# Two graph attention layers in one kernel: order of the first loads, four key buffers, a diagonal made by GpSimd, and the last sums split between engines

## The chip, the cores and the metric

The kernel runs on one core of a Trainium2 chip. A core has a matrix engine (TensorE, "PE" in the profile), three engines for elementwise work (VectorE "DVE", ScalarE "ACT", GpSimd "POOL"), and SyncE ("SP"), which here only starts transfers. Each engine executes its own instructions in order and waits for others by semaphores. The metric is the time of the whole kernel on the device, in microseconds; the number compared is the median of several runs.

## The reference: what is computed

Input are 4096 nodes with 512 features, `x`, and an adjacency matrix of 4096 x 4096 zeros and ones. Two layers follow each other, each with a residual and a layer normalisation.

```python
# layer 0: graph attention, 4 heads of width 128
support = (x @ weight)                       # per head
logits  = f1[None, :] + f2[:, None]          # two scalars per node and head
w       = where(logits >= 0, logits, 0.2 * logits)
masked  = w * adjacency
attn    = softmax(where(masked != 0, masked, -1e30)) * (masked != 0)
x       = layernorm(x + attn @ support + bias + x @ proj_w + proj_b)

# layer 1: masked attention, 8 heads of width 64
adj     = maximum(adjacency, eye)            # every node sees itself
q, k, v = x @ Wqs, x @ Wks, x @ Wvs          # per head
scores  = q @ k.T / 8 + 0.01 * eye - 1e16 * (1 - adj)
x       = layernorm(x + sum over heads of softmax(scores) @ v @ Wo)
```

In layer 1 the kernel takes the exponential without a maximum and multiplies by the adjacency matrix afterwards. The term `0.01 * eye` together with `maximum(adjacency, eye)` then means that the mask holds exp(0.01) = 1.01005 on its diagonal.

## The kernel before, as far as the change touches it

All matrices are float32. Constants: `P = 128`, `G = 512` queries in a group, `NG = 8` groups, `NT = 32` tiles of 128 keys, `NP1 = 4` pairs of heads, `NB = 3` key tiles in a batch. A "pair" (g, m) below is one group of queries with one pair of heads; there are 32 of them, each with 32 units j (one key tile each).

The head: loads of the first group of x, of the two weights and of the small vectors, then the transposes of x.

```python
            load_x(0)                                     # four DMAs, SyncE's queue
            for c in range(KC):
                nc.scalar.dma_start(w_sb[c], weight[c * P:(c + 1) * P, :])
            for c in range(KC):
                nc.sync.dma_start(pw_sb[c], proj_w[c * P:(c + 1) * P, :])
            nc.sync.dma_start(uv[:, 0, :], on_all_partitions(weight_u, D))
            # ... three more small vectors, each spread over all partitions
            load_x(1)
            # ...
            def turn_x(g, c):
                # ...
                p = xp.tile([P, GT, P], F32, name="x_ps")          # two such PSUM tiles
                for t in range(GT):
                    nc.tensor.transpose(p[:, t, :], xs[g * GT + t][:, c * P:(c + 1) * P], ident)  # line 701
                # copy to xT: VectorE for odd c (line 704), ScalarE for even c (line 706)

            for c in range(KC):
                turn_x(0, c)
            for g in range(NG):
                for t in range(GT):
                    # s_ps = xT @ w_sb  (line 727, 4 steps)
                    # b_ps = xT @ pw_sb (line 733, 4 steps), then turn_x(g + 1, ...)
```

During that stage GpSimd narrows the adjacency matrix to bfloat16 by DMA, SyncE's queue transposes it by DMA (`stage`), and ScalarE narrows it once more to 8 bits (line 582).

Between the layers the keys and queries are made. A PSUM tile with two heads' results is copied to `kq` (keys by VectorE, line 927; queries by ScalarE, line 929) and stored to HBM:

```python
                    kq = sp.tile([P, HP, G], F32, name="kq")       # two buffers
                    if w is wk:
                        nc.vector.tensor_copy(kq, s)
                    else:
                        nc.scalar.activation(kq, s, AF.Copy, scale=float(KD) ** -0.5)
                    # two DMAs to HBM on SyncE's queue
```

The pair loop of layer 1. In each unit TensorE makes scores (line 904), ScalarE the exponential in PSUM (line 1018), VectorE the product with the mask (line 1021), TensorE the product with the values (line 1066), and GpSimd adds the weights up for the softmax's denominator (`q_sum`):

```python
        def finish_md(g, t):          # the mask of the four tiles with the diagonal
            if t == 0:
                mdt[g] = lp.tile([P, GT, G], F32, name="md", bufs=1)
            nc.scalar.activation(mdt[g][:, t, :], mask(g, g * GT + t), AF.Copy)    # line 883
            d = mdt[g][:, t, t * P:(t + 1) * P]
            nc.vector.tensor_tensor(d, d, ident_e, op=ALU.max)                     # line 885
        # called in unit (g, 0, 4 * (g - 1) + t), used in units (g, m, 4 * g + t)

            def weigh(g, m, j, s):
                # ... exp(s) in place
                p = wp.tile([P, HP, G], F32, name="p1", bufs=18)
                keep = mdt[g][:, j % GT, :] if j // GT == g else mask(g, j)
                nc.vector.tensor_tensor(p, s, keep[:, None, :].to_broadcast([P, HP, G]), op=ALU.mult)

            def add_up(g, m, j):
                # for every second j: a, b are the weights of j - 1 and j; i = j // 2, n = 16
                if i == 0:
                    later.at(1, first)                    # q_sum = a + b, GpSimd
                elif at_end and i >= n - 2:               # at_end: the last pair (7, 3)
                    last_sum.extend((a, b))
                elif i % 8 == 7 or at_end and i >= n - 4:
                    later.at(2, lambda: add(a))           # q_sum += a, GpSimd, line 1041
                    later.at(3, lambda: add(b))
                else:
                    later.at(2, lambda: nc.gpsimd.dma_start(a, b, accum_op=ALU.add))  # a += b by DMA
                    later.at(5, lambda: add(a))
```

`later.at(n, ...)` issues an instruction n batches later. `all_sums` adds tiles over the partitions by a product with ones (line 1072), `project` is the product with `Wo` (line 1110), `close1` adds the residual (line 1120), normalises and stores. The end of the kernel:

```python
            step([], None, None)
            later.step()
            step([], None, tiles[-5], 2)
            # ... PSUM tiles y_ps[0..3], den_ps
            project(*tiles[-4], y_ps[0], range(NP1 - 1))
            all_sums([q_sum.pop(pairs[-1])] + last_sum, den_ps[:, 0, :])   # q_sum and four tiles
            divide_at_once(*pairs[-1], den_ps[:, 0, :])     # reciprocals by VectorE, line 1102
            for n in range(GT):
                if n + 1 < GT:
                    project(*tiles[n + 1 - GT], y_ps[n + 1], range(NP1 - 1))
                project(*tiles[n - GT], y_ps[n], [NP1 - 1])
                # ... close1
```

Of the kernel before, what the change touches and what calls it, by code (L numbers as in the profile page):

```python
# [8 lines left out]
F32 = mybir.dt.float32  # L9
# [4 lines left out]
ALU = mybir.AluOpType  # L14
# [4 lines left out]
P = 128  # L19
# [410 lines left out]
def tile_gat_then_masked_attention(  # L430
# [16 lines left out]
    nc = tc.nc  # L447
# [4 lines left out]
    G = 512  # L452
    NG = N // G
    GT = G // P
# [24 lines left out]
    nc.gpsimd.memset(minus_half, -0.5)  # L479
    ones = const.tile([P, KD], F32, name="ones")  # L480
    nc.gpsimd.memset(ones, 1.0)
    ident_e = const.tile([P, P], F32, name="ident_e")
    nc.vector.tensor_scalar(ident_e, ident, 1.0100501670841679, None, op0=ALU.mult)
    most = const.tile([P, NG * NP1], F32, name="most")
    total = const.tile([P, NG * NP1], F32, name="total")

# [64 lines left out]
    with tc.tile_pool(name="l0", bufs=NG) as l0, \  # L551
# [71 lines left out]
        with tc.tile_pool(name="l0s", bufs=2) as sp:  # L623
# [11 lines left out]

            load_x(0)
            for c in range(KC):
                nc.scalar.dma_start(w_sb[c], weight[c * P:(c + 1) * P, :])
            for c in range(KC):
                nc.sync.dma_start(pw_sb[c], proj_w[c * P:(c + 1) * P, :])  # L640
            nc.sync.dma_start(uv[:, 0, :], on_all_partitions(weight_u, D))
            nc.sync.dma_start(uv[:, 1, :], on_all_partitions(weight_v, D))
            nc.sync.dma_start(bb[:, 0, :], on_all_partitions(bias, D))
# [51 lines left out]
            def turn_x(g, c):  # L695

                if c == 0:
                    xTs[g] = sp.tile([P, KC, G], F32, name="xT")
                p = xp.tile([P, GT, P], F32, name="x_ps")
                for t in range(GT):  # L700
                    nc.tensor.transpose(p[:, t, :], xs[g * GT + t][:, c * P:(c + 1) * P], ident)
                dst = xTs[g][:, c, :]
                if c % 2:
                    nc.vector.tensor_copy(dst, p.rearrange("p t r -> p (t r)"))  # L704
                else:
                    nc.scalar.activation(dst, p.rearrange("p t r -> p (t r)"), AF.Copy)

            for c in range(KC):
                turn_x(0, c)
            for g in range(NG):  # L710
                xg = [xs[g * GT + t] for t in range(GT)]
                xT = xTs.pop(g)
                if g == 0:
                    nc.gpsimd.tensor_add(bb[:, 0, :], bb[:, 0, :], bb[:, 1, :])
                for t in range(GT):
                    nc.gpsimd.tensor_tensor(xg[t], xg[t], bb[:, 0, :], op=ALU.add)
                fs[g] = l0.tile([P, 2, GT, H0], F32, name="f")
                s4 = sp.tile([P, GT, H0, W0], F32, name="s4")
                for t in range(GT):
                    i = g * GT + t  # L720
                    if t == 1 and g + 2 < NG:
                        load_x(g + 2)
                    for fn in beside.get(i, []):
                        fn()
                    s_ps = op.tile([P, G], F32, name="o_ps")
                    for c in range(KC):
                        nc.tensor.matmul(s_ps, xT[:, c, t * P:(t + 1) * P], w_sb[c],  # L727
                                         start=(c == 0), stop=(c == KC - 1))
                    if g + 1 < NG and t == GT - 1:
                        turn_x(g + 1, t)  # L730
                    b_ps = op.tile([P, G], F32, name="o_ps")
                    for c in range(KC):
                        nc.tensor.matmul(b_ps, xT[:, c, t * P:(t + 1) * P], pw_sb[c],
                                         start=(c == 0), stop=(c == KC - 1))
                    if g + 1 < NG and t < GT - 1:
                        turn_x(g + 1, t)
                    nc.scalar.activation(s4[:, t, :, 0:D0],
                                         s_ps.rearrange("p (h d) -> p h d", h=H0), AF.Copy)
                    for k in range(2):
                        prod = sp.tile([P, H0, D0], F32, name="prod")  # L740
                        nc.vector.tensor_tensor(prod, s4[:, t, :, 0:D0],
                                                uv[:, k, :].rearrange("p (h d) -> p h d", h=H0),
                                                op=ALU.mult)
                        nc.vector.tensor_reduce(fs[g][:, k, t, :], prod, AX.X, ALU.add)
                    base = sp.tile([P, D], F32, name="base", bufs=4)
                    nc.vector.tensor_tensor(base, b_ps, xg[t], op=ALU.add)
                    nc.sync.dma_start(base_d[i], base)
                    later.step()
                factors(g, s4)
# [115 lines left out]
    with wait_by_tile("l1", 1) as l1, wait_by_tile("l1a", 2) as lp, \  # L865
# [13 lines left out]
        def finish_md(g, t):  # L879

            if t == 0:
                mdt[g] = lp.tile([P, GT, G], F32, name="md", bufs=1)
            nc.scalar.activation(mdt[g][:, t, :], mask(g, g * GT + t), AF.Copy)
            d = mdt[g][:, t, t * P:(t + 1) * P]
            nc.vector.tensor_tensor(d, d, ident_e, op=ALU.max)  # L885

        def load_kv(g, m, c):
            kt[g, m, c] = lp.tile([P, 2 * G], F32, name="k_sb", bufs=3)
# [21 lines left out]
        with wait_by_tile("l1s", 2) as sp:  # L910
# [7 lines left out]
            def keys_or_queries(g, w, dst):  # L918
                for m in range(0, NP1, 2):
                    s = ps.tile([P, HP, G], F32, name="s_ps")  # L920
                    for n in range(2):
                        for c in range(KC):
                            nc.tensor.matmul(s[:, n, :], w[:, c, (m + n) * P:(m + n + 1) * P],  # L923
                                             xTs[g][:, c, :], start=(c == 0), stop=(c == KC - 1))
                    kq = sp.tile([P, HP, G], F32, name="kq")
                    if w is wk:
                        nc.vector.tensor_copy(kq, s)
                    else:
                        nc.scalar.activation(kq, s, AF.Copy, scale=float(KD) ** -0.5)  # L929
                    for n in range(2):  # L930
                        nc.sync.dma_start(dst[m + n][g // 2][:, g % 2, :] if w is wk
                                          else dst[m + n][g], kq[:, n, :])
                    later.step()
                    later.step()
# [53 lines left out]
        with wait_by_tile("l1w", 2) as wp, wait_by_tile("l1o", 1, space=PSUM) as op:  # L988
# [4 lines left out]
            units = [(g, m, j) for g, m in pairs for j in range(NT)]  # L993
            index = {u: n for n, u in enumerate(units)}

            def loads(u):

                n = index[u]
                g, m, j = u
                if j % CH == 0:  # L1000
                    if n + CH < len(units):
                        g1, m1, j1 = units[n + CH]
                        if j1 == 0:
                            load_q(g1, m1)
                        load_kv(g1, m1, j1 // CH)
                if m == NP1 - 1 and (g + 1) * G % W == 0 and g + 1 < NG and j % CJ == 0:
                    for c in ((0, 1) if j == 0 else (j // CJ + 1,) if j // CJ + 1 < NCJ else ()):
                        load_adjT((g + 1) * G // W, c)
                if m == 0 and g and j // GT == g - 1:
                    finish_md(g, j % GT)  # L1010

            def scores(g, m, j):
                loads((g, m, j))
# [11 lines left out]
            def add_up(g, m, j):  # L1025
# [16 lines left out]

                if i == 0:
                    later.at(1, first)
                elif at_end and i >= n - 2:
                    last_sum.extend((a, b))
                elif i % 8 == 7 or at_end and i >= n - 4:
                    later.at(2, lambda: add(a))
                    later.at(3, lambda: add(b))
                else:  # L1050
                    later.at(2, lambda: nc.gpsimd.dma_start(a, b, accum_op=ALU.add))  # L1051
                    later.at(5, lambda: add(a))
# [55 lines left out]
            def project(g, t, s, ms=range(NP1)):  # L1108
                for m in ms:
                    nc.tensor.matmul(s, on_t[g][:, m, t * P:(t + 1) * P], wo_sb[:, m, :],  # L1110
                                     start=(m == 0), stop=(m == NP1 - 1))
# [62 lines left out]
                load_y(*t)  # L1174
            step([], None, None)
            later.step()
            step([], None, tiles[-5], 2)
            y_ps = ps.tile([P, HP, G], F32, name="s_ps")
            den_ps = ps.tile([P, HP, G], F32, name="s_ps")
            o_ps = op.tile([P, 2, G], F32, name="o1_ps")  # L1180
            y_ps = [y_ps[:, 0, :], y_ps[:, 1, :], o_ps[:, 0, :], o_ps[:, 1, :]]
            project(*tiles[-4], y_ps[0], range(NP1 - 1))
            all_sums([q_sum.pop(pairs[-1])] + last_sum, den_ps[:, 0, :])
            divide_at_once(*pairs[-1], den_ps[:, 0, :])
            for n in range(GT):
                if n + 1 < GT:
                    project(*tiles[n + 1 - GT], y_ps[n + 1], range(NP1 - 1))
                project(*tiles[n - GT], y_ps[n], [NP1 - 1])
                if n == GT - 2:
                    all_ok = all_in_range()  # L1190
                close1(*tiles[n - GT], y_ps[n], 1)
                later.step()
# [40 lines left out]
```

## Time and profile before

| quantity | value |
|---|---|
| time, median of 3 runs | 3474.48 us (3465.94 to 3479.73) |
| span of the profiled run | 3467.4 us |
| TensorE busy | 3421.7 us, 99% |
| VectorE busy | 2396.2 us, 69% |
| GpSimd busy | 2019.3 us, 58%; 1593.9 of 1700 us from 1600 to 3300 us |
| ScalarE busy | 1874.0 us, 54% |
| transfers | 620.8 MB, 179 GB/s on average |

How to read the lines below. A line of the busy times gives engine, busy microseconds, share of the span and number of instructions. In the list of waits a line reads: waiting engine, what it was about to do and its line, the releaser and its line; then microseconds in total, how often, and the longest. In the timeline and in the chain a line begins with start and duration; a timeline line goes on with engine, line, operation, output and input, their sizes and how many instructions were merged; in brackets stand the idle time ahead and what ended it. The kernel's stages in this run: layer 0's own products to about 249 us, its attention to 1175 us, keys, queries and values of layer 1 to about 1510 us, the pair loop to 3418 us, and the tail.

### The profile page before, as it was taken

To read this page: it belongs to the slowest core of one execution; us is meant where nothing else is said; L and a number is where in the kernel's file an instruction comes from. 1 tells how busy PE (TensorE), PEld (TensorE's weight loads), DVE (VectorE), ACT (ScalarE), POOL (GpSimd) and SP (SyncE) were. 2 spreads that over 40 slices of the span, in tenths; PEclk is the share of its full clock that TensorE was granted. 3 is DMA by queue.
4 is the path that set the end of the run, shared out by engine and by line. 5 is a ranking of instruction groups with operands and counts; after the bars stand their busy time and mean duration, and the time that the engine had idled before them with its cause. 6 is when DMAs were issued, how large, how long until landed. Compare 5 with 4: busy or idle time off the path is not lost.

```text
span 3467.4 us, 64921 instructions
## 1 busy us (share of the span) xinstructions
PE 3421.7 (99%) x26666; PEld 1867.3 (54%) x26666; DVE 2396.2 (69%) x2512; ACT 1874.0 (54%) x2194; POOL 2019.3 (58%) x1452
## 2 busy tenths in 40 slices
PE   9999999999999999999999999999999999999997
PEld 4459999999999744443333333333333333333332
DVE  3469999898898500047787777767776777767774
ACT  1236877878876310035555555555555555555552
POOL 3330031040020100039999999999999999999996
PEclk9999999999999999999999999999999999999998
DMA  8988959779441432458978988788988889787884
GB/s 185 229 176 144 211 126 217 146 172 205 141 111 62 101 130 97 161 154 196 206 182 206 243 192 205 190 207 229 214 190 207 194 199 253 190 209 187 210 190 96
DMA packets 398162, 620.80 MB, mean 179 GB/s; under 512 B 165536, under 2 KB 243616, under 8 KB 396832
## 3 DMA queue, kind: packets, MB, share of 16 engines
q0 software_dynamic: 97360, 258.50, 41.1%
q1 hardware_dynamic: 299392, 355.97, 34.9%
q8 instruction: 211, 3.46, 0.4%
q10 hardware_dynamic: 1104, 2.10, 0.2%
q14 instruction: 95, 0.78, 0.1%
HBM read 315.87 MB, written 117.64 MB: 125 GB/s over the span
## 4 chain that ended last, share of the span: by engine, by line
PE 61%; POOL 1%; DVE 1%; issue 1%; ACT 0%; DMA 0%; SPq 0%; POOLq 0%; DVEq 0%; ACTq 0%
PE s_ps L904 25%; PE o_ps L1066 24%; PE s_ps L923 5%; PE s_ps L1110 3%; PE s_ps L951 3%; PE s_ps L1072 1%; POOL q_sum L1041 1%; DVE p L1021 1%; PE x_ps L951 0%; DVE md L885 0%; ACT s_ps L1018 0%; DMA k_sb<-k_d 0%; DVE r L1086 0%; PE o_ps L1110 0%; POOL on L1090 0%
## 5 line engine op out<-in xcount | busy, mean ns | idle before, releaser
L1041 POOL TENSOR_TENSOR q_sum<-q_sum,p 128x1024 f32<-128x1024 f32 x543 | 1386.9, 2554 | 60.5 <-DMA p<-p 37.9
L1018 ACT ACTIVATE s_ps<-s_ps 128x1024 f32<-128x1024 f32 x1021 | 969.3, 1010 | 700.2 <-PE s_ps L904 698.7
L1021 DVE TENSOR_TENSOR p<-s_ps,adjT 128x1024 f32<-128x1024 f32 x896 | 1043.1, 1216 | 406.4 <-ACT s_ps L1018 389.7
L904 PE MATMUL s_ps<-q_sb,k_sb 64*64 64x512 f32 x8192 | 947.5, 590 | 7.2 <-DVE p L1021 5.9
L1066 PE MATMUL o_ps<-p,v_sb 64*64 64x512 f32 x8192 | 944.2, 590 | 0.0
L855 PE MATMUL o_ps<-sup_t,p 128*128 128x129 f32 x8192 | 919.0, 275 | 0.0
L855 PEld LDWEIGHTS o_ps<-sup_t,p 128*128 128x128 f32 x8192 | 916.8, 192 | 0.0
L618 DVE SCALAR_TENSOR_TENSOR p<-fr_t,dj,az 128x1024 f32<-128x1024 f32 x512 | 653.6, 1285 | 82.3 <-PE o_ps L855 54.9
L609 ACT ACTIVATE z<-fr_t,f 128x1024 fp8e4<-128x1024 f32 x512 | 558.4, 1144 | 126.5 <-DVE az L613 126.2
L904 PEld LDWEIGHTS s_ps<-q_sb,k_sb 64*64 64x64 f32 x8192 | 314.6, 133 | 576.8 <-issue 449.7
L1066 PEld LDWEIGHTS o_ps<-p,v_sb 64*64 64x64 f32 x8192 | 313.5, 133 | 569.7 <-issue 558.9
L1051 POOL DMA_DIRECT2D p<-p x413 | 439.3, 1299 | 24.8 <-PE o_ps L1066 15.5
L819 POOL DMA_DIRECT2D agg<-base_d x32 | 28.7, 1205 | 515.4 <-ACT agg L807 515.2
L1037 POOL TENSOR_TENSOR q_sum<-p,p 128x1024 f32<-128x1024 f32 x32 | 76.0, 2374 | 301.1 <-DVE p L1021 301.1
L1021 DVE TENSOR_TENSOR p<-s_ps,md 128x1024 f32<-128x1024 f32 x128 | 150.5, 1216 | 61.8 <-ACT s_ps L1018 60.6
L613 DVE TENSOR_TENSOR az<-adjT,z 128x512 int32<-128x512 int32 x256 | 175.5, 686 | 1.8 <-ACT z L609 1.0
L582 ACT ACTIVATE adjT<-stage 128x1024 fp8e4<-128x1024 bf16 x128 | 130.7, 1050 | 58.5 <-DMA stage<-adj_d 58.5
L569 POOL COPY seen<-token 128x1 f32<-128x1 f32 x24 | 13.5, 563 | 251.7 <-DVE token L567 251.7
L957 DVE COPY vg<-s_ps 128x512 f32<-128x512 f32 x15 | 10.4, 691 | 207.8 <-ACT vg L953 207.8
L929 ACT ACTIVATE kq<-s_ps 128x1024 f32<-128x1024 f32 x16 | 16.4, 1023 | 191.7 <-PE s_ps L923 184.5
L727 PE MATMUL o_ps<-w_sb,xT 128*128 128x512 f32 x256 | 116.3, 597 | 1.3 <-DVE xT L704 1.3
L1086 DVE RECIPROCAL r<-den 128x128 f32<-128x128 f32 x124 | 116.4, 939 | 0.0
(99 smaller groups left out, 1832.7 us busy)
## 6 DMA issues: line engine op xcount, KB each, us to landing
p<-p POOLq DMA_DIRECT2D x413, 512.0 KB, 9.1
k_sb<-k_d SPq DMA_DIRECT2D x128, 512.0 KB, 7.9
v_sb<-v_d SPq DMA_DIRECT2D x128, 512.0 KB, 6.4
adj_d<-in_adj_dram POOLq DMA_DIRECT2D x32, 1024.0 KB, 14.5
sup_t<-sup_d SPq DMA_DIRECT2D x120, 258.0 KB, 8.4
adjT_d<-adjT SPq DMA_DIRECT2D x32, 512.0 KB, 4.5
fr_t<-fr_d SPq DMA_DIRECT2D x16, 1024.0 KB, 6.6
adjT<-adjT_d SPq DMA_DIRECT2D x32, 512.0 KB, 8.1
```

Source lines behind the costliest of these rows:

```text
L582: nc.scalar.activation(adjT[w, c][:, k, :], stage[w, c][:, k, :], AF.Copy, saturate=False)
L609: nc.scalar.activation(z[:, k, :], fr[:, 0, :], AF.Sign, bias=fs[j // GT][:, 0, (j + k) % GT, h:h + 1], saturate=False)
L613: nc.vector.tensor_tensor(az.bitcast(I32), adjT[w, j // CJ][:, j % CJ:j % CJ + 2, :].bitcast(I32), z.bitcast(I32), op=ALU.bitwise_and)
L618: nc.vector.scalar_tensor_tensor(p, fr[:, 1, :], dj[j // GT][:, j % GT, h:h + 1], az_t[w, h, j // 2][:, j % 2, :], op0=ALU.max, op1=ALU.mult)
L855: nc.tensor.matmul(o[t // BK][:, t % BK, :], p[:, t * P:(t + 1) * P], s, start=(j == 0 and t % BK == 0), stop=(j == NT - 1), skip_group_ch ...
L904: nc.tensor.matmul(s[c:c + MS, e, :], k[r, a + c:a + c + MS], qt[g, m][r, :], start=True, stop=True)
L923: nc.tensor.matmul(s[:, n, :], w[:, c, (m + n) * P:(m + n + 1) * P], xTs[g][:, c, :], start=(c == 0), stop=(c == KC - 1))
L1018: nc.scalar.activation(s, s, AF.Exp)
L1021: nc.vector.tensor_tensor(p, s, keep[:, None, :].to_broadcast([P, HP, G]), op=ALU.mult)
L1041: nc.gpsimd.tensor_tensor(q, q, p, op=ALU.add)
L1051: later.at(2, lambda: nc.gpsimd.dma_start(a, b, accum_op=ALU.add))
L1066: nc.tensor.matmul(o[c, n, :], v[r, j % CH, c], p[r, e, :], start=(j == 0), stop=(j == NT - 1))
```

## The change

It has four parts. The order of the first loads: w is loaded behind x on SyncE's queue, and proj_w on ScalarE's queue behind the first copy of the transposed x; two of the first four transposes go to PSUM tiles of another pool, so that they need not wait for a copy. The keys and queries get four buffers instead of two. The diagonal of the mask is set by GpSimd's selection instead of a maximum on VectorE, and a pair of heads ahead of its first use instead of four units ahead. In the last pair, the weights of the last ten key tiles are not added by GpSimd: VectorE adds eight of them into one, TensorE takes that one and the last two, and the projections of two output tiles instead of one are issued before those sums.

```diff
-    ident_e = const.tile([P, P], F32, name="ident_e")
-    nc.vector.tensor_scalar(ident_e, ident, 1.0100501670841679, None, op0=ALU.mult)
...
             load_x(0)
             for c in range(KC):
-                nc.scalar.dma_start(w_sb[c], weight[c * P:(c + 1) * P, :])
-            for c in range(KC):
-                nc.sync.dma_start(pw_sb[c], proj_w[c * P:(c + 1) * P, :])
+                nc.sync.dma_start(w_sb[c], weight[c * P:(c + 1) * P, :])
...
-                p = xp.tile([P, GT, P], F32, name="x_ps")
+                if g == 0 and c > 1:
+                    p = op.tile([P, G], F32, name="o_ps").rearrange("p (t r) -> p t r", t=GT)
+                else:
+                    p = xp.tile([P, GT, P], F32, name="x_ps")
...
             for c in range(KC):
                 turn_x(0, c)
+                if c == 0:
+                    for n in range(KC):
+                        nc.scalar.dma_start(pw_sb[n], proj_w[n * P:(n + 1) * P, :])
...
-            nc.vector.tensor_tensor(d, d, ident_e, op=ALU.max)
+            nc.gpsimd.affine_select(out=d, in_=d, compare_op=ALU.not_equal, base=0,
+                                    fill=1.0100501670841679, pattern=[[-1, P]],
+                                    channel_multiplier=1)
...
-                    kq = sp.tile([P, HP, G], F32, name="kq")
+                    kq = sp.tile([P, HP, G], F32, name="kq", bufs=4)
...
+            diagonal = {index[g - 1, NP1 - 1, 0] + (g + 1) * GT + t: (g, t)
+                        for g in range(1, NG) for t in range(GT)}
...
-                if m == 0 and g and j // GT == g - 1:
-                    finish_md(g, j % GT)
+                if n in diagonal:
+                    finish_md(*diagonal[n])
...
-                elif at_end and i >= n - 2:
+                elif at_end and i >= n - 5:
                     last_sum.extend((a, b))
-                elif i % 8 == 7 or at_end and i >= n - 4:
+                elif i % 8 == 7:
...
             step([], None, None)
             later.step()
+            for p in last_sum[1:-2]:
+                nc.vector.tensor_tensor(last_sum[0], last_sum[0], p, op=ALU.add)
             step([], None, tiles[-5], 2)
...
-            project(*tiles[-4], y_ps[0], range(NP1 - 1))
-            all_sums([q_sum.pop(pairs[-1])] + last_sum, den_ps[:, 0, :])
+            for n in range(2):
+                project(*tiles[n - GT], y_ps[n], range(NP1 - 1))
+            all_sums([q_sum.pop(pairs[-1]), last_sum[0]] + last_sum[-2:], den_ps[:, 0, :])
             divide_at_once(*pairs[-1], den_ps[:, 0, :])
             for n in range(GT):
-                if n + 1 < GT:
-                    project(*tiles[n + 1 - GT], y_ps[n + 1], range(NP1 - 1))
+                if n + 2 < GT:
+                    project(*tiles[n + 2 - GT], y_ps[n + 2], range(NP1 - 1))
```

## The prediction

> **What bounds the kernel now.** I read the page's busy times and 40 slices first, then the list of waits of TensorE, then the chain of waits in order of time, then the timeline where those two show a hole.
>
> ```profile
> PE 3421.7 (99%) x26666; PEld 1867.3 (54%) x26666; DVE 2396.2 (69%) x2512; ACT 1874.0 (54%) x2194; POOL 2019.3 (58%) x1452
> PE s_ps L1072 <- POOL q_sum L1041: 10.9, 1, 10.9
> PE x_ps L701 <- DMA x_sb<-in_x_dram: 7.5, 4, 4.3
> PE s_ps L904 <- DVE p L1021: 5.9, 4, 3.5
> PE x_ps L836 <- ACT x1T L841: 3.8, 3, 1.9
> ```
>
> TensorE is idle for only 3467.4 - 3421.7 = 45.7 us of the span. No other engine is near that, and the change takes no matrix product away, so nothing can bring more than these 45.7 us plus what hides inside "busy" (matmuls stretched by small waits or by a lower clock). The four waits shown are the largest: the tail (10.9), the head (7.5), and two in between. The three main parts of the change aim at the first three.
>
> The 5.9 us of the third wait understate that hole. The chain in order of time has one piece per pair of heads, the projection on line 1110, and its starts give the period:
>
> ```profile
> 1852.11 3.63 PE s_ps L1110 x8
> 1911.83 3.63 PE s_ps L1110 x8
> 1971.55 3.63 PE s_ps L1110 x8
> 2033.22 3.63 PE s_ps L1110 x8
> 2092.94 3.63 PE s_ps L1110 x8
> ```
>
> The period is 59.72 us; one is 61.67, so 1.95 was lost. Followed to the end, all periods are 59.72 but for 61.67, 61.29 (from 2212.38 to 2273.67), 60.97 (from 2452.83 to 2513.80) and 60.53 (from 3170.73 to 3231.26). Before 1852 there is no projection and the period is 1677.54 - 1621.45 = 56.09; the two periods to 1796.02 take 118.48, which is 6.30 too much. Sum of the losses: 6.30 + 1.95 + 1.57 + 1.25 + 0.81 = 11.9 us. The losing pairs are those with m = 0 of groups 1, 2, 3, 4 and 7, where `finish_md` makes the diagonal mask. The worst one:
>
> ```profile
> 1736.09 6.89 DVE L885 TENSOR_TENSOR md<-md,ident_e 128x128 f32<-128x128 f32 x3
> 1739.05 8.63 POOL L1041 TENSOR_TENSOR q_sum<-q_sum,p 128x1024 f32<-128x1024 f32 x3
> 1742.90 3.47 DVE L1021 TENSOR_TENSOR p<-s_ps,adjT 128x1024 f32<-128x1024 f32 x3
> 1744.17 4.63 PE L904 MATMUL s_ps<-q_sb,k_sb 64*64 64x512 f32 x24 [3.51 <-DVE p L1021]
> ```
>
> Three maxima on 128x128 take 6.89 us, though the fastest of the 32 took 0.276. One of them ran from 1739.01 to 1742.98, beside a GpSimd sum from 1739.05 to 1742.82. VectorE stands behind it, so its masking product and TensorE's next scores are late.
>
> The tail:
>
> ```profile
> 3417.62 17.96 POOL L1041 TENSOR_TENSOR q_sum<-q_sum,p 128x1024 f32<-128x1024 f32 x7
> 3435.64 1.94 PE L1072 MATMUL s_ps<-q_sum,ones 128*32 128x512 f32 x8 [10.92 <-POOL q_sum L1041]
> 3443.16 0.96 DVE L1102 RECIPROCAL r<-s_ps 128x128 f32<-128x128 f32 x1 [19.35 <-PE s_ps L1072]
> 3453.55 0.69 DVE L1120 TENSOR_TENSOR y<-y,o_ps 128x512 f32<-128x512 f32 x1 [0.91 <-PE o_ps L1110]
> ```
>
> When the last product is issued GpSimd still has seven sums in its queue; they end at 3435.58 and TensorE waits 10.92 us.
>
> **What the skill says.** "SBUF — State Buffer", section "Who interferes with whom": a VectorE instruction with two SBUF inputs excludes a GpSimd instruction that reads SBUF, each for its whole length; with one SBUF input it does not. The trace agrees: the diagonal's maximum (two SBUF inputs) ended within 0.2 us of the end of the sum beside it, while the 1021 product (PSUM and SBUF) keeps its 1216 ns with GpSimd busy over 90%. "TensorE: Matmul & The Clock Gate", section "Part 1: The HAM clock gate": an idle array falls to a lower clock and needs work to rise again. Agrees: the granted clock was 0.70 from 3420 to 3440 and the matmuls of `ones` on p took 872 ns, those on q_sum 619. "DMA: Bandwidth & Descriptors", section "Issuing engines are not separate DMA queues": loads issued by ScalarE and SyncE share the same 16 engines and interleave. Agrees: from 3 to 10 us they are full (shares 0.96 to 1.06, 352 to 406 GB/s) and the four tiles of x, which TensorE needs first, come one by one to 8.93 us between the weights.
>
> **Part 1, the diagonal.** 28 maxima leave VectorE's stream in the pair loop (4 more run before it), and 28 selections enter GpSimd's. The only selection in the trace (128x128, for `ident`) took 0.29 us, so a group costs GpSimd 1.2 us against 59.72 - 0.94 x 59.72 = 3.6 us it has free per pair (1593.9 busy of 1700). The place moves from 4 to 28 units ahead of use, a unit being about 59.72 / 32 = 1.87 us, so some 50 us ahead: a late selection harms nobody. The single md buffer is safe too: its old content was last used at j = 4g - 1 of that pair and is overwritten from j = 4g + 4. ScalarE's copies (0.62 each) move along, up to three in a batch of 5.15 us, where ScalarE has 1.6 to 2.3 us idle. I take all 11.9 back and charge 0.4 for GpSimd waiting for those copies: **-11.5**.
>
> **Part 2, the tail.** Of GpSimd's seven last sums four go (both tiles of j = 26/27, the second of 24/25, the merged one of 22/23), and a sum and a DMA before them. Three stay (those merged on j = 16 to 21), of 2.4 us each, and can start about 1 us earlier. VectorE gets seven sums of 128x1024. The trace has its 128x512 product of two SBUF inputs at 0.682 and the 1024-wide 618 at 1.285; I take 1.2. They stand behind the o_sb sum on line 1163 (3419.21 + 0.69 = 3419.9). By the lock they alternate with GpSimd: first VectorE sum after GpSimd's second (3421.1), to 3422.4; GpSimd's third to 3424.8; the second VectorE sum to 3426.0; five more to 3432.0. TensorE meanwhile has two projections and the sum of q_sum, to about 3428.4. After 3432.0 three tiles are to be added over the partitions: in the loop one costs 8 matmuls in 0.86 to 1.06 us, in the cold tail it was 5.67 / 4 = 1.42. I take 1.2, so 3.6: sums at 3435.8 instead of 3443.1, -7.3. From there to the end of the span were 24.2 us: four reciprocals and four normalisations on VectorE (about 4 x 1.24 + 4 x 1.56 + 1.2 = 12.4) beside projections on TensorE, of which three matmul steps (3 x 0.86 = 2.6) are now done earlier. VectorE's own 12.4 allow only part of it, I take 1.6. Together **-8.9**.
>
> **Part 3, the head.** With w behind x on one queue the 1.05 MB of x are all there when 1.05 MB have moved: by the rates of each microsecond 0.69 MB at 4.0 us, so 5.2 instead of 8.93; w is whole at 2.1 MB, about 7.8. The first L727 started 3.9 after the last x; two more PSUM tiles take away its 0.8 us wait for a buffer, so 5.2 + 3.1 = 8.3 against 12.81. But the loads stay the same five MB, proj_w now on the other queue, and before they ended with x's second group at about 17.6 us. TensorE's transposes of that group were at 20.53. So at most 20.5 - 17.7 = 2.8 of the 4.5 is kept. The stage to 250 us then loses 1.8 to late adjacency transposes (ScalarE waited 12.48 for one at 215), and an earlier TensorE meets them earlier: I charge 0.6. **-2.2**.
>
> **Part 4, four key buffers.** VectorE waited once 10.15 us for a kq buffer, up to 1201.85. TensorE was fully busy from 1185 to 1225, for three PSUM tiles covered it. The later holes (3.8 on line 836) end with ScalarE's x1T copies, which stand in its own order behind copies that wait for TensorE. So nearly nothing: **-0.3**.
>
> **Sum**: -11.5 - 8.9 - 2.2 - 0.3 = -22.9, so 3474.5 - 22.9 = 3451.6; I say **3451 us**.
>
> **Rivals.**
> First, GpSimd becomes the bound in the pair loop: it is at 94%, and a selection in its order must wait for ScalarE's copy. For it: sums already wait 37.9 us for the accumulating DMAs. Against: 18 p buffers are six batches of slack, and only seven of the 32 pairs get four selections each. If it came, 2 to 5 us of part 1 are lost: about 3455.
> Second, the lock moves into the tail: VectorE's seven sums and GpSimd's three need 8.4 + 7.2 us of one port. If GpSimd goes last each time, q_sum comes at 3434 and the tail gains 4 instead of 8.9: 3456. If VectorE is not held at all, its sums end at 3428.5 and the tail gains 12: 3448.
> Third, the head is hidden: the loads' bytes or the adjacency transposes take all of it back. For it: the engines of DMA were full to 17.5 us and again from 60 to 190. Then 3454. If nothing is taken back, 3449.
> Fourth, a neutral result: the holes are there, but something else ends last in the same places. For the diagonal the timeline speaks against it, since pairs without a held maximum lose nothing.
>
> **Range and chances.** Terms: diagonal -9 to -12, tail -4 to -12, head 0 to -4, keys 0 to -1. The three times before spread over 3465.9 to 3479.7, so the median itself may be off by 4 or so. I set 3441 to 3461. 2% are 69 us, more than TensorE's idle time and the losses hidden in it together, and no part can plausibly cost that much: same 0.985, faster 0.005, slower 0.01.
>
> **What would show it.** Diagonal: all projections 59.7 us apart, no 904 wait on 1021 in the pair loop, selections of some 0.3 us (longer when held). Tail: three GpSimd sums after the last product, seven VectorE sums of which one or two last 2 to 3.5 us, the wait of 1072 below 5. Head: first L727 near 8.3, transposes of the second group near 17.7, and where the layer's own loop starts (248.9) some 2 us earlier. Keys: no wait of line 927 for DMA, line 836 still near 3.8. Wrong would be: periods still above 60, reciprocals of the end after 3440 less the shift of the loop, or a gain of the head that is gone by 250 us.

## The result, and the profile after

| | before | after |
|---|---|---|
| time, median of 4 runs each | 3475.23 us (3465.94 to 3479.73) | 3453.8 us (3449.82 to 3456.09) |
| ratio, with 95% interval | | 0.9941 [0.9918, 0.9963] |
| span of the profiled run | 3467.4 us | 3450.5 us |
| TensorE idle in it | 45.7 us | 35.3 us (3450.5 - 3415.2) |

The ratio is worth 20.5 us (12.9 to 28.5). The median of the changed kernel is 2.8 us above the predicted 3451. Single executions of one kernel differ by more than that, so the sum proves little about its terms; those are read stage by stage below. In the changed kernel's text lines 700, 729 and 735 are the old 701, 727 and 733; 857 is 855, 838 is 836, 908 is 904, 927 is 923, 1030 is 1021, 1050 is 1041, 1075 is 1066, 1081 is 1072, 1111 is 1102, 1119 is 1110 and 1129 is 1120. Line 887 is the selection. In the kernels of the experiments the lines are shifted by a few more; the tiles' names tell which is meant.

The page's busy times of the changed kernel, in the same columns as before:

```profile
PE 3415.2 (99%) x26658; PEld 1867.1 (54%) x26658; DVE 2374.8 (69%) x2486; ACT 1873.5 (54%) x2194; POOL 2015.8 (58%) x1478
```

The waits of TensorE in the changed kernel:

```profile
PE x_ps L700 <- DMA x_sb<-in_x_dram: 4.9, 3, 3.6
PE x_ps L838 <- ACT x1T L843: 3.8, 3, 1.9
PE s_ps L1081 <- DVE p L1187: 2.9, 1, 2.9
PE o_ps L857 <- DVE p L616: 2.8, 1, 2.8
PE o_ps L729 <- ACT xT L705: 2.5, 1, 2.5
...
PE s_ps L908 <- DVE p L1030: 1.2, 2, 1.0
```

The wait for GpSimd in the tail fell from 10.9 to a wait of 2.9 for VectorE, and the wait of the scores from 5.9 to 1.2. The head's wait fell from 7.5 to 4.9, but two waits are new: 2.5 for ScalarE's copy of the transposed x, and 2.8 in layer 0's attention. The 3.8 of the value stage did not move.

Where the profiled pair gained, by the starts of the stages in the two timelines (each row is what one stretch lasts):

| stretch | before | after | difference |
|---|---|---|---|
| start to layer 0's attention | 248.9 | 246.2 | -2.7 |
| its attention, to the first keys | 926.6 | 930.2 | +3.6 |
| keys, queries, values | 330.9 | 330.9 | 0.0 |
| pair loop, to the first projection behind its last product | 1912.0 | 1902.8 | -9.2 |
| from there to the first reciprocal of the end | 24.7 | 17.3 | -7.4 |
| from there to the end | 24.2 | 23.0 | -1.2 |
| span | 3467.4 | 3450.5 | -16.9 |

The pair loop. The chain of waits in order of time has these projections:

```profile
1848.57 3.63 PE s_ps L1119 x8
1908.30 3.63 PE s_ps L1119 x8
1968.02 3.63 PE s_ps L1119 x8
2027.74 3.63 PE s_ps L1119 x8
```

From 1848.57 to 1968.02 are 119.45 us, two periods of 59.72, and the next period, which took 61.67 before, is 59.72 as well. Over the whole loop the losses, by the same reckoning as in the prediction, are 0.51, 1.21, 0.35 and 0.45 = 2.5 us instead of 11.9. The first two are in pairs that have no projection yet. The timeline of VectorE shows the larger one:

```profile
1835.77 2.36 DVE L1030 TENSOR_TENSOR p<-s_ps,adjT 128x1024 f32<-128x1024 f32 x2 [2.24 <-DMA p<-p]
1838.91 2.36 DVE L1030 TENSOR_TENSOR p<-s_ps,adjT 128x1024 f32<-128x1024 f32 x2 [0.79 <-DMA p<-p]
```

VectorE doesn't wait for ScalarE here, as it does elsewhere, but for a p buffer that comes back late from the accumulating DMAs and from GpSimd. Stretches of about one pair each, with busy time (and number of instructions) of TensorE, its weight loads, VectorE, ScalarE and GpSimd, then the granted clock, the DMA share and GB/s:

```profile
1676.00:1732.00 56.00, 56.00 (x524) 19.64 (x520) 41.02 (x38) 34.43 (x41) 54.00 (x37) 1.00 0.85 197
...
1789.00:1848.00 59.00, 58.02 (x540) 19.85 (x532) 41.31 (x38) 33.54 (x39) 57.49 (x35) 1.00 0.88 205
1848.00:1908.00 60.00, 60.00 (x536) 21.08 (x528) 42.94 (x41) 33.24 (x39) 56.33 (x38) 1.00 0.87 208
```

GpSimd is busy for 54.0 of 56 us in the first of these stretches, and has nearly 4 us free only from 1848 on, where a pair is longer by its projection.

The tail, in the timeline of the changed kernel:

```profile
3409.78 5.63 POOL L1050 TENSOR_TENSOR q_sum<-q_sum,p 128x1024 f32<-128x1024 f32 x2 [0.17 <-DMA p<-p]
3410.14 8.85 PE L1119 MATMUL s_ps<-wo_sb,on 128*128 128x512 f32 x20
3411.51 11.29 DVE L1187 TENSOR_TENSOR p<-p,p 128x1024 f32<-128x1024 f32 x7
3418.92 1.06 PE L1081 MATMUL s_ps<-q_sum,ones 128*32 128x512 f32 x8
3422.85 4.46 PE L1081 MATMUL s_ps<-p,ones 128*32 128x512 f32 x24 [2.87 <-DVE p L1187]
3427.45 0.96 DVE L1111 RECIPROCAL r<-s_ps 128x128 f32<-128x128 f32 x1 [3.12 <-PE s_ps L1081]
```

One of the three sums that GpSimd keeps is over at 3409.61, before the last product; GpSimd is done with the other two at 3415.41, before TensorE asks for q_sum. TensorE then stands for VectorE's seven sums, which end at 3422.80. The group of these sums, with the shortest, median and longest in ns:

```profile
L1187 DVE TENSOR_TENSOR p<-p,p x7: 1225/1226/3253, 3411.5 to 3421.6; 128x1024 f32<-128x1024 f32 x7
```

Five last 1.23 us. The first lasts 1.70, from 3411.51, and ends 1.08 us after GpSimd's sum beside it; the second lasts 3.25, from 3413.24, and ends 1.08 us after GpSimd's last.

### The profile page after: what moved, and what is told of

The parts are those of the page before. It is cut to its first block, busy times and chain, and to the rows that moved or that the text cites. A ratio compares the mean times of both kernels' runs of the same rounds, so it can differ in the third digit from the quotient of the medians.

```text
span 3450.5 us, 64904 instructions
## 1 busy us (share of the span) xinstructions
PE 3415.2 (99%) x26658; PEld 1867.1 (54%) x26658; DVE 2374.8 (69%) x2486; ACT 1873.5 (54%) x2194; POOL 2015.8 (58%) x1478
## 4 chain that ended last, share of the span: by engine, by line
PE 87%; issue 4%; DMA 3%; POOL 3%; DVE 1%; ACT 1%; SPq 0%; POOLq 0%; ACTq 0%; DVEq 0%
PE o_ps L857 25%; PE o_ps L1075 24%; PE s_ps L908 23%; PE s_ps L927 6%; PE s_ps L955 3%; PE s_ps L1119 3%; DMA stage<-adj_d 2%; POOL q_sum L1050 1%; DMA p<-p 1%; PE s_ps L1081 1%; PE o_ps L729 1%; PE o_ps L735 1%; POOL x_sb L718 1%; POOL s L662 0%; PE x_ps L838 0%
## 5 line engine op out<-in xcount | busy, mean ns | idle before, releaser
L1060 POOL DMA_DIRECT2D p<-p x412 | 439.4, 1307 | 21.1 <-PE o_ps L1075 20.2
L611 DVE TENSOR_TENSOR az<-adjT,z 128x512 int32<-128x512 int32 x256 | 175.6, 686 | 12.3 <-ACT z L607 11.8
L887 POOL TENSOR_SCALAR_AFFINE_SELECT md<-md 128x128 f32<-128x128 f32 x32 | 18.6, 911 | 265.6 <-ACT md L885 265.6
L580 ACT ACTIVATE adjT<-stage 128x1024 fp8e4<-128x1024 bf16 x128 | 130.7, 1050 | 60.8 <-DMA stage<-adj_d 60.8
L567 POOL COPY seen<-token 128x1 f32<-128x1 f32 x24 | 12.9, 539 | 251.1 <-DVE token L565 251.1
L961 DVE COPY vg<-s_ps 128x512 f32<-128x512 f32 x15 | 10.4, 692 | 209.3 <-ACT vg L957 209.3
```

The source lines that it names most:

```text
L611: nc.vector.tensor_tensor(az.bitcast(I32), adjT[w, j // CJ][:, j % CJ:j % CJ + 2, :].bitcast(I32), z.bitcast(I32), op=ALU.bitwise_and)
```

## The experiments

Each ratio is to the kernel before on the same chip, with its 95% interval. The medians of the kernel before were 3471.42 us for the first four kernels, 3477.98 for the next four and 3478.91 for the last four. The ratios are not the quotients of the two medians: for the diagonal alone the medians are 6.9 us apart and the ratio is worth 11.5.

**The diagonal alone.** The kernel before with the selection and its new place:

```diff
-            nc.vector.tensor_tensor(d, d, ident_e, op=ALU.max)
+            nc.gpsimd.affine_select(out=d, in_=d, compare_op=ALU.not_equal, base=0, ...)
...
-                if m == 0 and g and j // GT == g - 1:
-                    finish_md(g, j % GT)
+                if n in diagonal:
+                    finish_md(*diagonal[n])
```

> The kernel before with the diagonal's part alone (GpSimd's selection, a pair of heads ahead). Theory, held maxima on VectorE were the loss: the pair loop loses 2.5 us or less to its even periods instead of some 12, the tail stays as before (line 1072 waits near 11 us), time -9 us, ratio 0.9974. Rival, GpSimd is the bound at the end, so a faster loop only makes the tail's wait longer by as much: wait of 1072 near 18 to 20, time -1 to -3.

Measured: 3464.56 us, 0.9967 [0.9956, 0.9977], or -11.5 us (-8.0 to -15.3). The pair loop lost 0.68 us in all. The wait list of TensorE shows that the tail took none of it back, for its wait is the 10.9 of before:

```profile
PE s_ps L1077 <- POOL q_sum L1046: 10.9, 1, 10.9
```

So the holes of the diagonal are worth what their sum in the periods said, and an earlier loop moves the whole tail with it.

**The tail alone.** The four edits of the last pair in the kernel before, of which the core is:

```diff
-                elif at_end and i >= n - 2:
+                elif at_end and i >= n - 5:
...
+            for p in last_sum[1:-2]:
+                nc.vector.tensor_tensor(last_sum[0], last_sum[0], p, op=ALU.add)
```

> The kernel before with the tail's part alone. Theory: from the last product with values to the first reciprocal of the end 17.3 us instead of 24.7, time -8.5 us, ratio 0.9975; the pair loop keeps losses of about 12 us. Rival, VectorE and GpSimd exclude each other for the whole of both lists: seven VectorE sums take over 14 us, time -4.

Measured: 3466.81 us, 0.9981 [0.9970, 0.9992], or -6.6 us (-2.8 to -10.4). From the last product to the first reciprocal are 17.2 us (3417.75 to 3434.92), against 24.7 before and 17.3 in the whole change: the tail's stretch is the same alone and together. VectorE's seven sums take 11.24 us, and TensorE waits 2.8 us for them. The pair loop, not touched, lost 12.84 us, as before.

**The head alone.** The three edits of the loads and transposes:

```diff
-                nc.scalar.dma_start(w_sb[c], weight[c * P:(c + 1) * P, :])
-            for c in range(KC):
-                nc.sync.dma_start(pw_sb[c], proj_w[c * P:(c + 1) * P, :])
+                nc.sync.dma_start(w_sb[c], weight[c * P:(c + 1) * P, :])
...
+                if c == 0:
+                    for n in range(KC):
+                        nc.scalar.dma_start(pw_sb[n], proj_w[n * P:(n + 1) * P, :])
```

> The kernel before with the new order of the first loads alone. Theory, the gain is there but taken back by a stage paced by other things: layer 0's attention starts near 246.2 instead of 248.9, layer 1's keys start near 1176 as before, time 0 us within 1.5. Rival, what was lost again in the changed kernel between 398 and 403 us (2.8 us, TensorE waiting for VectorE) was an accident of that execution: keys start near 1172.8, time -2.7, ratio 0.9992.

Measured: 3475.95 us, 1.0004 [0.9992, 1.0017], or +1.4 us (-2.8 to +5.9): no gain that can be measured. Two timelines of this kernel show why, first that of TensorE, then that of ScalarE with its queue:

```profile
9.56 1.92 PE L731 MATMUL o_ps<-w_sb,xT 128*128 128x512 f32 x4
15.29 2.67 PE L731 MATMUL o_ps<-w_sb,xT 128*128 128x512 f32 x4 [3.81 <-ACT xT L707]
17.76 4.65 PE L737 MATMUL o_ps<-pw_sb,xT 128*128 128x512 f32 x8
```

```profile
8.75 5.85 ACTq L713 DMA_DIRECT2D pw_sb<-in_L_gnn_proj_w_dram  x4
14.64 0.60 ACT L707 ACTIVATE xT<-o_ps 128x512 f32<-128x512 f32 x1 [6.80 <-DMA bb<-in_L_gnn_proj_b_dram]
```

Here the first product starts at 9.56 instead of 12.81, but after the first half TensorE stands for the third copy of x, which is ScalarE's. ScalarE issues the four loads of proj_w from 8.75 to 14.60, and its copy stands in order behind them. (The bracket names a DMA of another tensor; the issue ends 0.04 us before the copy begins, so I take it that the issue held it.) After the wait the granted clock was 0.50 from 17 to 19 us, and the eight products with proj_w took 4.65 us where they took 3.92 in the changed kernel. In the changed kernel the same issue takes 4.58 us, from 8.46 to 13.04, and the wait is the 2.5 of its list.

In this execution TensorE also lost 5.5 us at 371 us, in layer 0's attention, where loads stand behind late transposes of the adjacency. Layer 0's attention starts at 248.9, as before the change, and the keys at 1184.3, 8.7 later: neither the theory's 246.2 and 1176 nor the rival's 1172.8 came. I come back to that.

**The keys alone.**

```diff
-                    kq = sp.tile([P, HP, G], F32, name="kq")
+                    kq = sp.tile([P, HP, G], F32, name="kq", bufs=4)
```

> The kernel before with four buffers for keys and queries alone. Theory, three PSUM tiles covered VectorE's wait: no wait of line 927 for DMA under 1205 us, line 836 still waits near 3.8 us, time 0 us. Rival, the late normalisations behind that wait caused line 836's waits: these fall under 1 us and time is -3.

Measured: 3474.32 us, 1.0010 [0.9995, 1.0024]. The wait of line 836 is 3.8, three times, the longest 1.9, to the digit as before, though line 927's wait of 10.2 us for DMA is gone.

**The two halves of the diagonal.** First the selection by GpSimd at its old place, four units ahead of use (the engine alone); then VectorE's maximum at the new place, a pair ahead (the place alone). The edits are the first and the second half of the diff of the diagonal.

> The kernel before with GpSimd's selection in place of VectorE's maximum, but still four units ahead of use. Theory, the lock that holds VectorE's maximum is the loss and the engine is what matters: the pair loop loses 1 to 4 us instead of 12, time -8 to -11, ratio near 0.997. Rival, the place matters (GpSimd's queue makes a selection four units, some 7.5 us, ahead too late): VectorE's masking product waits for selections, the loop loses 8 or more, time -3 or less.

> The kernel before with VectorE's maximum kept, but a pair of heads ahead. Theory, the maximum is held wherever it stands, and what it costs depends on how much else VectorE has in those batches: by the losses of before at the same units (6.3 at units 0 to 3, 1.95, 1.57, 1.25, 0, 0, 0.81 for the next fours) the loop loses 10 to 12 us, time -1, ratio 0.9995. Rival, the short distance to use was the loss: the loop loses under 3, time -9.

Measured: engine alone 3472.13 us, 0.9980 [0.9967, 0.9993], the loop lost 4.7 us; place alone 3467.98 us, 0.9979 [0.9967, 0.9991], the loop lost 6.4 us. Of the 11.9 us the engine alone gives back 7.2 and the place alone 5.5, each about half; in time they are worth 7.0 (2.4 to 11.5) and 7.3 (3.1 to 11.5). The engine alone fell a little short of its theory (a loss of 1 to 4), and that the place alone would give next to nothing was wrong. The engine alone, by the instructions on the mask tile (shortest, median and longest in ns; then what VectorE's masking product waited for, us and times):

```profile
L883 POOL TENSOR_SCALAR_AFFINE_SELECT md<-md x28: 287/583/1925, 1742.7 to 3227.7; 128x128 f32<-128x128 f32 x28
...
  ACT s_ps L1018: 57.6, 35
  POOL md L883: 12.3, 7
```

Four units are too few for an engine that is busy 94% of the time: the selection stands behind sums in GpSimd's order, and VectorE waits 12.3 us for it, part of which reaches TensorE. The place alone, same view:

```profile
L885 DVE TENSOR_TENSOR md<-md,ident_e x28: 227/636/3094, 1690.7 to 3178.6; 128x128 f32<-128x128 f32 x28
```

The maximum is still held behind GpSimd's sums, up to 3.09 us, but nothing needs its result soon. Its losses (3.1 in the fourth period, then 1.3, 1.2, 0.8) sit in other pairs than before. Why half of the holds then do no harm these runs don't settle.

**Everything but the head, and the changed kernel again.** The first keeps the loads as before and has the other three parts.

> The changed kernel with the first loads as they were before. Theory, the new loads gain 2.7 us by 246 us and the slower adjacency transposes in layer 0's attention take them back: attention to keys takes 926.7 us here, time as the changed kernel's within 2 us, ratio 0.994. Rival, the new loads' gain lasts in most executions: ratio 0.9949, 2.7 us slower than the changed kernel beside it.

> The changed kernel once more, beside the three others. Theory: ratio 0.994; attention to keys again longer than 926.7 us by 2 to 9 us, because the new loads shift the adjacency transposes. Rival, the stall near 400 us was an accident: attention to keys 926.7 us.

Measured, beside each other, with six runs each: without the head 3456.22 us, 0.9944 [0.9923, 0.9964]; the changed kernel 3462.27 us, 0.9946 [0.9926, 0.9966]. The head adds nothing that the timing shows. Attention to keys took 929.1 us without the head, with 2.2 us of waiting that the theory did not have, and 936.7 with it, 10.0 over the 926.7 where the theory had 2 to 9. In the profiled execution of the changed kernel its stretch to the first keys was 1189.1 us, where the first one had 1176.5: that one execution was luckier at the front. The pair loop lost 1.25 us without the head and 0.75 with it.

**proj_w on SyncE's queue.** The changed kernel, with ScalarE freed of the issue:

```diff
+            for c in range(KC):
+                nc.sync.dma_start(pw_sb[c], proj_w[c * P:(c + 1) * P, :])
...
-                if c == 0:
-                    for n in range(KC):
-                        nc.scalar.dma_start(pw_sb[n], proj_w[n * P:(n + 1) * P, :])
```

> The changed kernel, but proj_w is loaded on SyncE's queue behind w, so that ScalarE does not stand at its issue. Theory, the 4.6 us of issuing were what delayed the third copy of x (13.1 us): TensorE's first eight products no longer wait 2.5 us, the second group's transposes come at 17.5 to 18 instead of 19.3, layer 0's attention starts near 245, time 0 to -1.5. Rival, the loads' bytes decide: the transposes stay at 19 or later, because x's second group is now behind proj_w.

Measured: 3455.61 us, 0.9944 [0.9922, 0.9966], no better than the changed kernel. TensorE's timeline:

```profile
10.49 4.09 PE L728 MATMUL o_ps<-w_sb,xT 128*128 128x512 f32 x8
14.42 3.60 PE L734 MATMUL o_ps<-pw_sb,xT 128*128 128x512 f32 x8
19.26 0.30 PE L702 MATMUL x_ps<-ident,x_sb 128*128 128x128 f32 x1 [1.25 <-DMA x_sb<-in_x_dram]
19.83 0.33 PE L702 MATMUL x_ps<-ident,x_sb 128*128 128x128 f32 x1 [0.27 <-DMA x_sb<-in_x_dram]
```

The wait for the copy is gone, all eight first products run on, and now the second group's transposes wait for x, one load after the other, the last at 21.14. So both are true: ScalarE's issue costs 2.5 to 3.8 us, and without it x's second group, now behind proj_w on the one queue, comes later and takes the same time back. The DMA engines are busy for 0.99 of the time from 4 to 18 us; whether their bytes or the order in the queue holds x is not separated here. Layer 0's attention started at 253.2, where the theory had 245.

**Fewer sums by VectorE.** The changed kernel, with TensorE taking the last four tiles instead of two (five sums by VectorE), and with TensorE taking all ten (none by VectorE); nothing is left out of the sum:

```diff
-            for p in last_sum[1:-2]:
+            for p in last_sum[1:-4]:
...
-            all_sums([q_sum.pop(pairs[-1]), last_sum[0]] + last_sum[-2:], den_ps[:, 0, :])
+            all_sums([q_sum.pop(pairs[-1]), last_sum[0]] + last_sum[-4:], den_ps[:, 0, :])
```

> The changed kernel, but VectorE adds six tiles into one (five sums) and TensorE takes that one, the last four and q_sum. Theory, the seven sums are what TensorE waits for (2.9 us) and two of them, not held, are 2.4 us: VectorE's sums end 2.4 us earlier, TensorE has two more tiles (1.7 us) but waits under 1 us and its clock stays up; from the last product to the first reciprocal 15 us instead of 17.3, time -2. Rival, TensorE bounds the tail already: 17.5 to 19, time 0 to +2.

> The changed kernel, but no tile is added by VectorE: TensorE takes q_sum and all ten tiles. Theory, eleven tiles at 0.86 to 1.06 us after the projections: no wait, GpSimd's three sums of 2.4 us each unheld, 18.5 us from the last product to the first reciprocal, so 1 us slower than the changed kernel and still 6 better than before. Rival, the sums of tiles at 1.4 us each, as in the cold tail of before: 23 us or more, most of the tail's gain lost.

Measured: five sums 3461.77 us, 0.9948 [0.9933, 0.9963]; no sums 3465.66 us, 0.9963 [0.9952, 0.9975]. The timelines of TensorE, five sums first:

```profile
3428.44 4.50 PE L1081 MATMUL s_ps<-p,ones 128*32 128x512 f32 x40 [0.33 <-DVE p L1187]
```

```profile
3420.98 8.77 PE L1081 MATMUL s_ps<-p,ones 128*32 128x512 f32 x80
```

Five tiles take 4.50 us (0.90 each) and ten 8.77 (0.88), while three took 4.46 in the changed kernel (1.49 each). The stretches that hold these sums differ in the granted clock (the third figure from the end), changed kernel first, then five sums:

```profile
3422.80:3427.30 4.50, 4.45 (x25) 0.99 (x25) 1.47 (x3) 0.00 (x0) 1.22 (x4) 0.62 0.00 0
```

```profile
3427.30:3435.00 7.70, 7.37 (x53) 2.25 (x46) 4.45 (x7) 0.00 (x0) 1.22 (x4) 1.00 0.00 0
```

After its 2.87 us of waiting TensorE got 0.62 of its clock; without that wait it kept 1.00. The fall does not follow every time. Of five executions with seven sums, four show it, with three tiles in 4.38 to 4.48 us; the kernel without the head waited as long and kept 1.00:

```profile
3422.31 2.78 PE L1077 MATMUL s_ps<-p,ones 128*32 128x512 f32 x24 [2.81 <-DVE p L1183]
```

From the last product to the first reciprocal: 14.8 us with five sums, 18.6 with none, 17.3 with seven (15.6 where the clock stayed up). Five is the better split in the traces, by 2.5 or 0.8 us; the timing, 0.9948 against 0.9946 for the changed kernel above, does not show it.

**Both improvements together**, proj_w on SyncE and five sums:

> Both: proj_w on SyncE's queue and five VectorE sums in the tail. Theory: -2 to -3.5 us against the changed kernel beside it, ratio 0.993 to the kernel before. Rival: the two changes are below what the spread of executions lets through, ratio 0.994.

Measured: 3461.44 us, 0.9956 [0.9939, 0.9972]. Its stretch to the first reciprocal is 14.8 again, but the interval overlaps that of the changed kernel: the -2 to -3.5 of the theory is not shown, and no version here is shown to beat the changed kernel.

## The prediction, step by step

**The diagonal, -11.5: right.** The loop gained 11.9 - 0.7 = 11.2 with this part alone. That the time came out at -11.5 as well is luck to the tenth, since its interval runs from -8.0 to -15.3; with all parts on, the loop lost 0.02 to 2.5 us in the executions seen. GpSimd's selection costs what `ident`'s did: where it follows a sum it lasts 0.30 us, and the next sum starts 0.26 us after it. Its median of 0.92 us in the loop is no lock: such a record starts while a DMA issue ahead of it on the same engine still runs (one at 1705.81, issues of 1.75 us from 1704.65). The scores' wait for line 1030 fell from 5.9 to 1.2, and what is left of it has another cause, next.

The rival of GpSimd as the bound came true in small, and its "against" had one wrong size. I took 3.6 us free per pair from a mean over the loop; in the first five pairs the period is 56.09, and in the stretches of the third and fourth GpSimd is busy for 53.5 and 54.0 of 56, so 2 to 2.5 are free. There the changed kernel lost 1.7 us in one execution, and less in others.

**The tail's sums, -7.3: right to 0.1, with two terms that were off by under 1 us each way.** VectorE's sums took 11.3 us from the end of the o_sb sum where I had 12.1 (3419.9 to 3432.0). A free one costs 1.23 (I took 1.2), and two were held by GpSimd, for 0.5 and 2.0 us: that is the alternation that the prediction worked out by the rule of the Trainium skill, "SBUF — State Buffer", section "Who interferes with whom", and the trace agrees with it. The rival without a lock gave 12 us and fell; so did the one in which GpSimd goes last, for it ended 7.4 us before VectorE. The three tiles then took 4.46 us where I had 3.6: I had allowed for a lower clock, but not by enough. At full clock they would cost 3 x 0.90 = 2.7, and without the fall of the clock they took 2.78. That the two errors cancel to 0.1 is luck: where the clock stayed up, the same stretch was 15.6 us, a gain of 9.1. The wait I put below 5 was 2.9. From there to the end it was -1.2 against -1.6. The timing of the tail alone, -6.6 with an interval to -10.4, agrees.

**The keys, -0.3: right**, as nothing. The early wait for the kq buffers' DMA is gone, line 836's stays.

**The head, -2.2: wrong.** Its first half held: the first product came at 9.17 where I had 8.3 and before had 12.81. The step that failed is "transposes of the second group near 17.7", and with it "at most 2.8 of the 4.5 is kept": they came at 19.33 in the changed kernel. Over all profiled executions of kernels that differ in this:

| start, us | old loads, 7 executions | new loads, 5 | new, proj_w on SyncE, 2 |
|---|---|---|---|
| second group's first four transposes | 19.7 to 21.1, mean 20.5 | 19.3 to 23.5, mean 21.5 | 19.3, 18.4 |
| second group's next four | 27.0 to 28.4, mean 27.9 | 26.6 to 30.8, mean 28.8 | 29.9, 28.8 |
| layer 0's attention | 246.5 to 248.9, mean 247.8 | 246.2 to 253.2, mean 250.0 | 253.2, 251.0 |
| layer 1's keys | 1174.0 to 1179.1, mean 1175.6 | 1176.5 to 1189.1, mean 1183.4 | 1182.9, 1188.0 |

By the second four nothing is left of the 3.6 us that the first product gained; the mean is 1.0 us worse. I had counted the bytes of the loads and not the engine that issues them: ScalarE stood 4.6 and 5.9 us over four loads, in the changed kernel and with the head alone, with a copy behind them. The 17.7 was itself too early in all but one execution: it is when the DMA engines had moved the bytes, but before the change the last load of x's second group, issued at 12.39, took 6.8 us to land, to 19.2. With the new loads it landed between 17.3 and 19.2, so without ScalarE's hold I estimate that 1.3 to 3.2 us (20.5 less these) could have been kept. Where the hold is mended that load lands at 21.1 and 20.2 and the gain is gone again, as the third rival ("the head is hidden") had it.

To layer 0's attention the mean is 2.2 us worse and to the keys 7.8. The larger part of that lies in layer 0's attention, which lasted 926.6 to 932.7 us with the old loads and 927.2 to 937.4 with the new. These are single executions with at most a few waits each, and such waits are seen without the new loads too: 2.9 us before line 853 with the engine alone, which cost 6.0 in all, for the granted clock was 0.50 behind it, and 2.2 with everything but the head. Nor do the means compare like with like: the seven executions with the old loads were all 5.3 to 8.1 us faster than their kernels' medians, the five with the new between 10.6 faster and 1.9 slower. The timing of the head alone leaves room for a loss of up to 5.9 us. Whether the new loads make the later stalls likelier stays open.

The 2.7 us that the first profiled execution had at 246 us would have passed for the predicted 2. It was not repeated, and layer 0's attention took 3.6 back in the same execution.

**The sum.** With the head at 0 instead of -2.2 the terms make -20.7, and the timing -20.5. The parts alone make -11.5 - 6.6 + 1.4 + 3.5 = -13.2, each uncertain by 4 or 5 us; the 7.3 between that and -20.5 are within what these and the whole's own 8 us add up to, so no interplay of the parts is shown.

## What to carry to other kernels

Where one engine is busy 99% of the span, look for periods longer than the others and sum what they lose: here that sum was 11.9 us, and the loop gained 11.2 when their cause was gone. A load was there when it landed, some 1.5 us after the DMA engines ran empty (19.2 against 17.6): an estimate from bytes and rates has to add that. A load costs its issuing engine time too: before moving loads to another queue, read how long that queue stands at such an issue, and what stands behind it in order. When an engine is to take in new work, take its free time from the tightest stretch, not from a mean, and give it work that is due long after.

## What was not expected of the hardware

- After a wait of 2.87 us TensorE's granted clock was 0.62 over the next 4.5 us; five tiles without the wait took as long as three after it. The Trainium skill, "TensorE: Matmul & The Clock Gate", section "Part 1: The HAM clock gate", speaks of about 3.4 us of idle; in four of five executions waits of 2.82 to 2.97 us sufficed, in the fifth 2.81 did not. The length of the wait does not decide alone: at 12 to 16 us waits of 3.59 and 3.69 us, with all ten and with four tiles given to TensorE, left the clock at 1.00, and with the head alone 3.81 was followed by 0.50.
- Four loads of 256 KB, issued by ScalarE, held its queue for 4.58 us in one kernel and 5.85 in another; before, SyncE issued the same four in 2.05 us, from 4.37, and behind w on one queue in 3.48. The DMA engines were full each time, so what lengthens the issue is not shown.
- GpSimd's records overlap: a selection that follows a DMA issue shows up to 1.99 us, one that follows a sum 0.30.
